# Mixture-of-experts rows: from accumulating scatters into HBM to slot-ordered writes with gathers by node

## The chip, the core and the metric

The kernel runs on one core of a Trainium2 chip. The metric is device time in microseconds (us) of one execution; three executions of the kernel before had a median of 1533.02 us (1530.13 to 1534.28). The inputs are fixed by a seed: 625 nodes with 512 features, 10,000 edges, and about 160 MB of weights and rows moved from HBM in one execution. All arithmetic of the routed layers is float32.

## The reference

Four pairs of a graph layer and a mixture-of-experts layer ("ffn") are applied to the node rows `x`, each added to its input. Two of the expert layers, called L1 and L3, are of concern here. In both each node goes to its two best of eight experts, and the two outputs are summed with a weight per choice:

```python
# L1: relu expert, 512 -> 1024 -> 512, softmax over the two best
topk_vals, topk_idx = jax.lax.top_k(logits, K)
topk_weights = jax.nn.softmax(topk_vals, axis=-1)
h = jax.nn.relu(jnp.einsum('bsh,ehf->bsef', x, w1) + b1)
expert_out = jnp.einsum('bsef,efh->bseh', h, w2) + b2
...
# L3: silu-gated expert, 512 -> 1536 -> 512, gates renormalised over the two best
out = out + combine[:, e:e + 1] * (h @ w2[e].T)
```

After L1 come a layer norm and the graph layer L2. After L3 the kernel ends: `x + L3_ffn` is its output.

## The kernel before, in words

Nodes lie in five tiles of T = 125 rows (`NT` = 5). The experts are ranked by how many nodes chose them; `CAPS` gives a fixed capacity to each rank, and every (node, choice) pair gets a *slot*, in blocks of B = 128 slots. Blocks beyond the capacities ("overflow", up to `NO`) are worked on inside nested runtime branches `tc.If(n_over[0] > i)` (L1054); in this execution none is taken. `ITEMS` lists in which order a layer works through its ranks: in L1 rank 4, 0, then 5 and 6 merged in one block of two 64-slot halves, then 1, 2, 3, 7; in L3 rank 4, 0, 1, 2, 3, 5, 6, 7. Both layers have 13 ordinary blocks (`OVER`).

`routed` (L791) runs one such layer. `dispatch` (L640) computes slots, the node of every slot (`node`) and, by ten one-hot matmuls (L764), the gate of every slot (`gate`). Then for each item: `fetch` (L872) gathers the block's rows from HBM (`rows_hbm`) with an indirect DMA on POOL's queue; `enter` (L890) transposes them on the tensor engine; `hidden` (L899, or `hidden2` L939 for the merged item) is the first product with its activation; `back` (L995) the second. An item whose width is a multiple of 128 gets its output rows straight from `back` (L1036); for the others the output comes transposed (L1003) and `turned` (L1012) turns it, one block after each step of the *next* item's `hidden`. The weights, 1 MB a chunk, stream through a ring of nine buffers: `refill` (L863) on SP's queue brings chunk n when chunk n - 9 has been read.

What the change is about is where a block's output rows go. `give` (L976) lets DVE scale them by the slot's gate into one of two buffers `ys_out` (L981), and then issues on POOL's queue an indirect DMA that *adds* the rows to the nodes' rows in HBM (L985):

```python
nc.vector.tensor_scalar(y[:n], ps[:n, 0, :], over[0][:n, b:b + 1], None, op0=OP.mult)
...
nc.gpsimd.indirect_dma_start(
    out=sums[layer], in_=y[:n], in_offset=None, compute_op=OP.add, ...)
```

All these scatters write one HBM tensor, so each waits for the one before. `keep` (L1087) first puts `x` there. In L1 that tensor is `sums`, and after the layer L1684 and L1685 read it back to `x` tile by tile, `LayerNorm.add` (L328) and `close` (L345) normalise it, and `to_features` (L388) feeds L2's first matmuls (`mm_nodes`, L455); 24 idle matmuls (`warm(24)`, L1679, which the trace shows as 48 records) keep the tensor engine busy meanwhile. In L3 the tensor is the kernel's output itself.

The order of the instructions on an engine is made by a scheduler when the program is built: of the instructions that its own cost estimates hold to be ready it takes the one that comes first in the program. On the chip each engine then runs its list strictly in order. `tc.issue_after(i)` forces instructions behind `i` on its engine. A `tc.If` is a fence for the scheduler: nothing crosses it. PSUM has four buffers of two banks.

Of the kernel before, what the change touches and what calls it, by code (L numbers as in the profile page):

```python
# [11 lines left out]
F32 = mybir.dt.float32  # L12
# [7 lines left out]
P = 128  # L20
# [27 lines left out]

ITEMS = {"L1": ((4,), (0,), (5, 6), (1,), (2,), (3,), (7,)),
         "L3": ((4,), (0,), (1,), (2,), (3,), (5,), (6,), (7,))}  # L50
# [145 lines left out]
def kernel(  # L196
# [443 lines left out]
    def dispatch(layer, o12, weigh, w0, per, dp, oh0):  # L640

        mask = dp.tile([T, NT, E], BF16, tag="mask", name="mask")
        nc.vector.tensor_add(mask, o12[:, 0], o12[:, 1])
# [99 lines left out]
        nc.vector.tensor_scalar(free, one, 0.0, spare, op0=OP.is_equal, op1=OP.mult)  # L746
        node = small.tile([P, NB], I32, tag="node", name="node")
        node_made = nc.vector.scalar_tensor_tensor(node, one, -1.0, free, op0=OP.add, op1=OP.add)
        yield node

        with tc.issue_after(node_made.ins):
            g12 = weigh()

            rest = dp.tile([T, 2 * NT], F32, tag="rest", name="rest")
            nc.vector.tensor_copy(rest, g12.rearrange("p c t -> p (c t)"))
            gates = dp.tile([T, 2 * NT, 3, NB], BF16, tag="gates", name="gates")
            piece = dp.tile([T, 3, 2 * NT], BF16, tag="piece", name="piece")
            for i in range(3):
                nc.vector.tensor_copy(piece[:, i, :], rest)
                if i < 2:  # L760
                    nc.vector.tensor_sub(rest, rest, piece[:, i, :])
                nc.vector.tensor_mul(gates[:, :, i, :], ohb, bcast(piece[:, i, :], NB))
        for n in range(2 * NT):
            pe["last"] = nc.tensor.matmul(ps[:, 1, :3 * NB], ohp[:, n, :],  # L764
                                          gates[:, n].rearrange("p i b -> p (i b)"),
                                          start=(n == 0), stop=(n == 2 * NT - 1))
        gate = small.tile([P, NB], F32, tag="gate", name="gate")
        last = nc.vector.tensor_reduce(gate, ps[:, 1, :3 * NB].rearrange("p (i b) -> p b i", b=NB),
                                axis=AX.X, op=OP.add)
        with tc.issue_after(last.ins):  # L770

            nc.vector.tensor_add(ovb, ovb, nov)
            le = dp.tile([P, NO, E], F32, tag="le", name="le")
            nc.vector.tensor_tensor(le, ovb[:, None, :].to_broadcast([P, NO, E]),
                                    blk[:, :NO, None].to_broadcast([P, NO, E]), op=OP.is_le)
            own = dp.tile([P, NO], F32, tag="own", name="own")
            nc.vector.tensor_reduce(own, le, axis=AX.X, op=OP.add)
            nc.vector.tensor_scalar(own, own, float(E - 1), None, op0=OP.min)
            whose = small.tile([P, NO, E], F32, tag="whose", name="whose")
            nc.vector.tensor_tensor(whose, own[:, :, None].to_broadcast([P, NO, E]),  # L780
                                    eio[:, None, :].to_broadcast([P, NO, E]), op=OP.is_equal)
            routing[layer, "over"] = small.tile([1, NO + 1], I32, tag="ovr_i", name="ovr_i")
            nc.vector.tensor_scalar(routing[layer, "over"][:, :NO], own[0:1, :], float(per),
                                    float(w0), op0=OP.mult, op1=OP.add)
            nc.vector.tensor_copy(routing[layer, "over"][:, NO:], ovb[0:1, E - 1:])
        pe["picked"] = last
        yield gate, whose

    HALVES = (slice(0, B // 2), slice(B // 2, B))

    def routed(layer, lg, rows, nch, nw, activate, vectors=lambda *_: None, rest=lambda *_: ()):  # L791

# [9 lines left out]
        with tc.tile_pool(name=f"{layer}w", bufs=1) as more, \  # L802
# [15 lines left out]
            yT = rpool.tile([P, KD, tall], F32, name="yT")  # L818
            beyond = rpool.tile([P, 2], I32, name="beyond")
            nc.gpsimd.memset(beyond, 0)  # L820
            nc.gpsimd.memset(beyond[B // 2:, 0:1], 2 * N)
            nc.gpsimd.memset(beyond[:B // 2, 1:2], 2 * N)
            brought, counts = {"n": 0}, {"xg": 0, "y": 0}
# [110 lines left out]
            def bias_of(i, m=0):  # L934
                if i < ni:
                    return vectors(ranks[:, :, items[i][m]], pool)
                return vectors(over[1][:, i - ni, :], pool)

# [36 lines left out]

            def give(b, n, ps, parts=None, later=None):  # L976


                y = ys_out[counts["y"] % len(ys_out)]
                counts["y"] += 1  # L980
                nc.vector.tensor_scalar(y[:n], ps[:n, 0, :], over[0][:n, b:b + 1], None, op0=OP.mult)  # L981

                def added():
                    for at_nodes in parts or (nodes[0][:n, b:b + 1],):
                        nc.gpsimd.indirect_dma_start(  # L985
                            out=sums[layer], in_=y[:n], in_offset=None, compute_op=OP.add,
                            out_offset=bass.IndirectOffsetOnAxis(ap=at_nodes, axis=0),
                            bounds_check=N - 1, oob_is_err=False)

                if later is None:  # L990
                    added()
                else:
                    later.append(added)

            def back(i, between):  # L995
# [25 lines left out]
                else:  # L1021
                    for m, (b, rows) in enumerate(blocks(i)):
                        ps = pstile("ps_y")
                        for f in range(nf):
# [13 lines left out]
                            if m == n // B - 1:  # L1038
                                done(i, f)
                        if i < ni and len(items[i]) > 1:  # L1040

                            by_half = pool.tile([P, 2], I32, tag="half", name="half")
                            nc.vector.tensor_tensor(by_half,
                                                    nodes[0][:, b:b + 1].to_broadcast([P, 2]),
                                                    beyond, op=OP.add)
                            give(b, rows, ps, [by_half[:, j:j + 1] for j in range(2)])
                        else:
                            give(b, rows, ps, later=todo if i == 0 else None)
                return todo

            def overflow(i):

                if i < NO:
                    with tc.If(n_over[0] > i):  # L1054
                        enter(ni + i)
                        if i + 1 < NO:
                            fetch(ni + i + 1)
                        hidden(ni + i, [])
                        back(ni + i, [])
                        overflow(i + 1)  # L1060

            n_over, over = [], []
            warm(4)
            o12, g12, weigh = choose(lg)
            oh0 = yT.rearrange("p k s -> p (k s)")[:T, :NT * B].rearrange("p (t s) -> p t s", t=NT)
            steps = dispatch(layer, o12, weigh, w0, per, dp, oh0)
# [11 lines left out]
            def weights_of_blocks():  # L1078
# [5 lines left out]
                after.pop(0)() if after else None  # L1084
                after.append(keep)

            def keep():  # L1087
                for part, hbm in by_node(sums[layer]):
                    nc.scalar.dma_start(hbm, x[part])

            after = []
            todo = [None, None, rows_of_others, None, weights_of_blocks]
            for i in range(ni):
                hidden(i, todo)
                ahead = [lambda: enter(i + 1), lambda: fetch(i + 2)] if i + 1 < ni else []
                todo = back(i, ahead)
                if i == 0:
                    todo = after + todo
            assert not todo
            pe["picked"] = None  # L1100
            overflow(0)
        state["stop"] = len(plan)

# [321 lines left out]
    rows_hbm = tc.dram_tile([N + B, D], F32, name="rows_hbm")  # L1425
    sums = {"L1": tc.dram_tile([N, D], F32, name="sums"), "L3": out}
    with tc.tile_pool(name="empty", bufs=1) as pool:
        empty = pool.tile([B, D], F32, name="empty")
        nc.gpsimd.memset(empty, 0.0)
        nc.gpsimd.dma_start(rows_hbm[N:N + B, :], empty)  # L1430

    prio = const.tile([T, E], F32, name="prio")
# [244 lines left out]

    routed("L1", lg, xn, 2, 1, l1_activate, l1_vectors, l1_rest)
    warm(24, behind=False)  # L1679
    xn = ktile("xn")  # L1680
    ln = LayerNorm(xn, groups=GROUPS)
    for t in range(NT):
        hbm = sums["L1"][t * T:(t + 1) * T, :]
        nc.sync.dma_start(x[:112, t, :], hbm[:112, :])  # L1684
        nc.scalar.dma_start(x[112:T, t, :], hbm[112:T, :])  # L1685
        ln.add(t, x[:, t, :])
    xnT = to_features(xn, "xnT")

# [102 lines left out]

    routed("L3", lg, xn, 3, 2, l3_activate)

# [30 lines left out]
```

## Time and profile before

| | |
|---|---|
| median of 3 runs | 1533.02 us (1530.13 to 1534.28) |
| the profiled execution | 1532.33 us, of which its span is 1530.5 us |
| TensorE busy / mean granted clock | 94% of the span / 0.978 |
| DVE, ACT, POOL busy | 43%, 25%, 14% |
| L1 routed, with its selection | about 714 to 915 us of the span |
| L3 routed, with its selection | about 1126 us to the end |
| scatters (L985) | 27, median 5.8 us from issue to landing |
| gathers of rows (L876) | 26, median 7.3 us |

PE is the tensor engine's matmuls, PEld its weight loads, DVE the vector engine, ACT the scalar engine, POOL the GpSimd engine, SP the sync engine; a q behind a name (SPq) means the engine's queue. A row of the timeline reads: start, duration, engine, line, operation, output<-input, shape, count; in brackets how long the engine was idle before it and what ended the idle time. An fp32 matmul shows as two records, so counts of records are twice the counts in the code.

### The profile page before, as it was taken

The numbers are of one execution on the slowest core, as the hardware profiler recorded it, in microseconds if no ns is written. First come the engines' busy times: TensorE is split into PE (matmuls) and PEld (weight loads), VectorE is DVE, ScalarE is ACT, GpSimd is POOL, SyncE is SP. The second block draws the span as 40 slices with busy tenths as digits, with TensorE's granted clock in tenths as the row PEclk, the third lists the DMA queues.
The fourth block names the chain that finished last, engine by engine and source line by source line (L and its number), as shares of the span: only waits on it lengthen the run. The fifth ranks groups of instructions, "written<-read, shape, count | busy, mean of one in ns | idle before, by whom it ended". The sixth has DMA issues, their size and how long they took to land.

```text
span 1530.5 us, 18483 instructions
## 1 busy us (share of the span) xinstructions
PE 1442.2 (94%) x7068; PEld 1011.3 (66%) x7068; DVE 660.9 (43%) x1752; ACT 388.6 (25%) x768; POOL 215.7 (14%) x355
## 2 busy tenths in 40 slices
PE   9998999999999999987998999799979999999996
PEld 6775556647566655655655886555558668999885
DVE  9845563372985538747411115846362101111100
ACT  2223272121564126622110105512131000011000
POOL 1010041300242013400212111100001001101000
PEclk9999999999999999998999999899989999999998
DMA  4010100021100110001966523000039416457880
GB/s 151 12 35 30 67 15 28 28 83 33 50 1 1 55 55 1 1 1 62 396 220 224 170 37 128 28 28 28 0 127 409 180 67 209 156 185 265 300 295 4
DMA packets 29057, 159.41 MB, mean 104 GB/s; under 512 B 4073, under 2 KB 4201, under 8 KB 12065
## 3 DMA queue, kind: packets, MB, share of 16 engines
q1 hardware_dynamic: 20791, 141.56, 25.2%
q0 software_dynamic: 5424, 11.32, 3.4%
q10 hardware_dynamic: 2746, 5.25, 1.1%
q8 instruction: 59, 0.97, 0.3%
q14 instruction: 37, 0.30, 0.1%
HBM read 166.49 MB, written 11.58 MB: 116 GB/s over the span
## 4 chain that ended last, share of the span: by engine, by line
PE 73%; DVE 10%; DMA 6%; issue 6%; ACT 4%; POOL 0%; SPq 0%; ACTq 0%; POOLq 0%; DVEq 0%
PE ps_h L916 16%; PE ps_mf L447 14%; PE ps_mn L455 7%; PE ps_y L1003 7%; PE ps_s L1165 5%; DMA sums<-slots,node 5%; PE ps_o L1229 4%; PE ps_eo L1119 4%; PE ps_a L1332 3%; PE ps_p L1208 3%; PE ps_mg L436 3%; PE ps_y L1036 2%; DVE s L1171 1%; PE ps_tr L397 1%; DMA slots<-rows_hbm,node 1%
## 5 line engine op out<-in xcount | busy, mean ns | idle before, releaser
L916 PE MATMUL ps_h<-xgT,ring 128*128 128x128 f32 (+5 forms) x1920 | 322.4, 328 | 4.0 <-DVE slots L981 3.9
L916 PEld LDWEIGHTS ps_h<-xgT,ring 128*128 128x128 f32 x1920 | 278.3, 192 | 45.5 <-issue 6.8
L1194 POOL TENSOR_SCALAR s<-s,rs 125x625 f32<-125x625 f32 (+4 forms) x120 | 96.3, 818 | 309.3 <-DVE rs L1191 286.6
L1003 PE MATMUL ps_y<-hT,ring 128*128 128x352 f32 (+4 forms) x640 | 137.0, 373 | 0.0
L1003 PEld LDWEIGHTS ps_y<-hT,ring 128*128 128x128 f32 x640 | 108.7, 190 | 24.3 <-issue 0.2
L1790 DVE TENSOR_TENSOR hT<-ps_h,g 128x512 f32<-128x512 f32 (+4 forms) x60 | 27.8, 464 | 197.4 <-ACT g L1789 191.0
L1176 ACT ACTIVATE s<-s,mn 125x626 f32<-125x626 f32 (+4 forms) x120 | 87.4, 745 | 62.1 <-DVE mn L1171 62.1
L1171 DVE CUSTOM_DVE_ANT_0 s<-ps_s,mask 125x626 f32<-125x626 f32 (+4 forms) x120 | 82.1, 718 | 31.7 <-PE ps_s L1165 30.8
L1165 PE MATMUL ps_s<-kT,qT 64*125 64x313 f32 (+4 forms) x416 | 84.5, 458 | 5.1 <-DVE mn L1171 5.1
L1789 ACT ACTIVATE g<-ps_h 128x512 f32<-128x512 f32 (+4 forms) x60 | 25.0, 417 | 250.7 <-PE ps_h L916 250.7
L876 POOL DMA_INDIRECT slots<-rows_hbm,node x26 | 25.5, 980 | 375.1 <-PE ps_x L894 198.1
L1208 PEld LDWEIGHTS ps_p<-ident,s 125*125 125x125 f32 x432 | 53.0, 192 | 29.1 <-issue 15.0
L1186 DVE SCALAR_TENSOR_TENSOR s<-s,cnt 125x626 f32<-125x626 f32 x80 | 66.2, 846 | 12.3 <-ACT s L1176 12.2
L1119 PE MATMUL ps_eo<-w,h 128*125 128x512 f32 x160 | 70.5, 593 | 0.6 <-ACT h L1115 0.6
L1229 PE MATMUL ps_o<-pT,v 125*64 125x375 f32 (+2 forms) x448 | 60.2, 413 | 9.1 <-DVE mn L1171 4.7
L1208 PE MATMUL ps_p<-ident,s 125*125 125x125 f32 x432 | 63.8, 290 | 4.2 <-DVE mn L1171 1.7
L1165 PEld LDWEIGHTS ps_s<-kT,qT 64*125 64x125 f32 x416 | 43.7, 186 | 32.2 <-DVE mn L1171 11.8
L386 PE MATMUL ps_warm<-rows,ident 128*128 128x313 f32 x202 | 60.4, 455 | 1.0 <-DVEq L1054 1.0
L1036 PE MATMUL ps_y<-ring,hT 128*128 128x512 f32 x128 | 58.3, 605 | 0.0
L1332 PE MATMUL ps_a<-dst,src 125*128 125x313 f16 x400 | 54.9, 297 | 1.4 <-DVE dst L1318 1.0
L1119 PEld LDWEIGHTS ps_eo<-w,h 128*125 128x125 f32 x160 | 29.8, 188 | 36.4 <-issue 30.9
L455 PE MATMUL ps_mn<-w,hxT 128*125 128x512 f32 x120 | 52.0, 593 | 0.6 <-ACT hxT L277 0.6
(414 smaller groups left out, 1978.6 us busy)
## 6 DMA issues: line engine op xcount, KB each, us to landing
ring<-in_weights SPq DMA_DIRECT2D x122, 1024.0 KB
w<-in_weights SPq DMA_DIRECT2D x27, 1024.0 KB
rows_hbm<-xn ACTq DMA_DIRECT2D x2, 1120.0 KB
x<-in_x SPq DMA_DIRECT2D x1, 1120.0 KB
sums<-x ACTq DMA_DIRECT2D x1, 1120.0 KB
x<-sums SPq DMA_DIRECT2D x5, 224.0 KB
out<-x ACTq DMA_DIRECT2D x1, 1120.0 KB
rows<-in_rows SPq DMA_DIRECT2D x1, 1052.0 KB
```

The lines of the kernel that those rows point to most:

```text
L447: pe["last"] = nc.tensor.matmul(ps[:, half, :HC], w, r[:, half * HC:(half + 1) * HC], start=(n == 0), stop=(n == last))
L455: pe["last"] = nc.tensor.matmul(ps[:T, 0, :width], src[:, k, t * T:(t + 1) * T], w[:, k, :width], start=(k == 0), stop=(k == KD - 1 and ex ...
L916: pe["last"] = nc.tensor.matmul(ps[:, m, g * n:(g + 1) * n], w[:, k, j * P:(j + 1) * P], xgT[:, k, :n], start=(k == 0), stop=(k == KD - 1))
L1003: nc.tensor.matmul(ps[:, 0, :n], second(i, f)[:, d * P:(d + 1) * P], hT[:, f, :n], start=(f == 0), stop=(f == nf - 1))
L1036: nc.tensor.matmul(ps[:, 0, :], hT[:, f, m * B:m * B + rows], second(i, f), start=(f == 0), stop=(f == nf - 1))
L1119: pe["last"] = nc.tensor.matmul(ps[:T, 0, :], hs[e][:, t * T:(t + 1) * T], ws[e // 4][1][:, e % 4, :], start=True, stop=True)
L1165: nc.tensor.matmul(ps[hh][:T, i, :w], qT[rr, b, t * T:(t + 1) * T], kT[rr, b, i * w:(i + 1) * w], start=True, stop=True)
L1171: nc.vector.tensor_tensor_reduce(s[:, hh, :nb * w].rearrange("p (a c) -> p a c", a=nb), ps[hh][:T, :nb, :w], mask[:, t, :nb * w].rearrange ...
L1194: nc.gpsimd.tensor_scalar(s[:, hh, :w], s[:, hh, :w], rs[:, hh:hh + 1], 1.0, op0=OP.mult, op1=OP.mult)
L1208: nc.tensor.transpose(pp[:T, hh, j * T:(j + 1) * T], s[:, hh, j * T:(j + 1) * T], ident[:T, :T])
L1229: nc.tensor.matmul(po[rr, 0, o:n * T], v[:, j, h * DH:(h + 1) * DH], pT[:, hh, j, o:n * T], start=(j == 0), stop=(j == nk - 1))
L1332: nc.tensor.matmul(pa[b // 2][:, b % 2, :HC], srcs[c % SRCS][:, b, :], dsts[c][:, :HC], start=(c == c0), stop=(c == c1 - 1))
```

## The change

Routed outputs no longer go through accumulating scatters.

- **Ordinary blocks but the last.** `give` copies the rows unscaled on ACT to `ys_out`, and an ordinary DMA on ACT's queue writes them to `ys_hbm` at the block's slots.
- **Nodes fetch theirs.** Before the last item's `hidden`, `picked_up` issues ten indirect gathers on POOL (five node tiles by two choices, 125 rows each) from `ys_hbm`, and DVE adds each to `x` with the node's gate. A choice that lies in the last block or in overflow is pointed at a row of zeros. In L1 the last two of the ten additions are held back until `spread`.
- **The last block (and overflow).** `one_hots` builds five 128 x 125 one-hot matrices on DVE; `spread` multiplies each with the block's rows on the tensor engine (K = 128, 512 columns), and DVE adds the product, times the gate, to `x`. The call for the last ordinary block stands behind the overflow branches.
- **After a node tile is complete** a callback runs: in L1 its layer-norm statistics (tiles 0 and 2 on ACT, the others on DVE), in L3 the DMAs of the tile to the output. `keep` and the reading back of `sums` are gone; `warm(24)` becomes `warm(4)`.
- **In `dispatch`** the three-piece gates, their ten matmuls and the reduction are gone; a clamped slot number, one product and one sum come in.
- **Order.** In L1 the merged item (5, 6) moves from third to sixth place. Overflow rows are fetched inside the branch. At the program's start ten small DMAs on POOL put zeros to the unused rows of `ys_hbm`.

```diff
-ITEMS = {"L1": ((4,), (0,), (5, 6), (1,), (2,), (3,), (7,)),
+ITEMS = {"L1": ((4,), (0,), (1,), (2,), (3,), (5, 6), (7,)),
...
-        for n in range(2 * NT):
-            pe["last"] = nc.tensor.matmul(ps[:, 1, :3 * NB], ohp[:, n, :],
-                                          gates[:, n].rearrange("p i b -> p (i b)"),
-                                          start=(n == 0), stop=(n == 2 * NT - 1))
-        gate = small.tile([P, NB], F32, tag="gate", name="gate")
...
+            nc.vector.tensor_scalar(from_hbm, slot, B * (OVER[layer] - 1), None, op0=OP.min)
...
+            nc.vector.tensor_mul(by_choice, ohb[:, :, late],
+                                 bcast(g12.rearrange("p c t -> p (c t)"), NO + 1))
+            gate = small.tile([T, NT, NO + 1], F32, tag="gate", name="gate", bufs=1)
+            last = nc.vector.tensor_add(gate, by_choice[:, :NT, :], by_choice[:, NT:, :])
...
-            def give(b, n, ps, parts=None, later=None):
+            def give(b, n, ps):
                 y = ys_out[counts["y"] % len(ys_out)]
-                counts["y"] += 1
-                nc.vector.tensor_scalar(y[:n], ps[:n, 0, :], over[0][:n, b:b + 1], None, op0=OP.mult)
...
+                if b < over0:
+                    counts["y"] += 1
+                nc.scalar.copy(y[:n], ps[:n, 0, :])
+                if b < over0 - 1:
+                    nc.scalar.dma_start(ys_hbm[layer][B * b:B * b + n, :], y[:n])
                 else:
+                    kept.append((b, y))
+
+            def picked_up():
...
+                for n in order:
+                    nc.gpsimd.indirect_dma_start(
+                        out=places[n], out_offset=None, in_=ys_hbm[layer],
+                        in_offset=bass.IndirectOffsetOnAxis(ap=over[0][:, n:n + 1], axis=0))
+                def add(n):
+                    c, t = divmod(n, NT)
+                    nc.vector.scalar_tensor_tensor(x[:, t, :], places[n], weights_of[0][:, c, t:t + 1],
+                                                   x[:, t, :], op0=OP.mult, op1=OP.add)
+                for n in order[:-2]:
+                    add(n)
+                return [lambda n=n: add(n) for n in order[-2:]]
+
+            def one_hots(b):
...
+                for t in range(NT):
+                    nc.vector.tensor_scalar(ohT[:, t, :], place[:, :T], float(t * T), number,
+                                            op0=OP.add, op1=OP.is_equal)
+                return ohT
+
+            def spread(ohT, remain=(), done=lambda t: None):
+                b, y = kept.pop()
+                for t in range(NT):
+                    ps = pstile("ps_sp")
+                    pe["last"] = nc.tensor.matmul(ps[:T, 0, :], ohT[:, t, :], y, start=True, stop=True)
+                    if t == NT - 1 and remain:
+                        with tc.issue_after(last.ins):
+                            while remain:
+                                remain.pop(0)()
+                    j = b - over0 + 1
+                    last = nc.vector.scalar_tensor_tensor(x[:, t, :], ps[:T, 0, :], over[1][:, t, j:j + 1],
+                                                          x[:, t, :], op0=OP.mult, op1=OP.add)
+                    done(t)
...
             for i in range(ni):
+                if i == ni - 1:
+                    assert not todo
+                    remain = picked_up()
+                    if nw > 1:
+                        while remain:
+                            remain.pop()()
+                    ohT = one_hots(over0 - 1)
                 hidden(i, todo)
...
             overflow(0)
+            kept.append(last)
+            spread(ohT, remain, lambda t: complete(t, spares[0][:, t, :]))
...
-    warm(24, behind=False)
-    xn = ktile("xn")
-    ln = LayerNorm(xn, groups=GROUPS)
-    for t in range(NT):
-        hbm = sums["L1"][t * T:(t + 1) * T, :]
-        nc.sync.dma_start(x[:112, t, :], hbm[:112, :])
-        nc.scalar.dma_start(x[112:T, t, :], hbm[112:T, :])
-        ln.add(t, x[:, t, :])
+    def l1_complete(t, spare):
+        if t == 0:
+            l2["xn"] = ktile("xn")
+            l2["ln"] = LayerNorm(l2["xn"], groups=GROUPS)
+        l2["ln"].add(t, x[:, t, :], t in (0, 2), spare)
+
+    routed("L1", lg, xn, 2, 1, l1_activate, l1_complete, l1_vectors, l1_rest)
+    warm(4)
...
+    def l3_complete(t, _):
+        hbm = out[t * T:(t + 1) * T, :]
+        nc.sync.dma_start(hbm[:112, :], x[:112, t, :])
+        nc.scalar.dma_start(hbm[112:, :], x[112:T, t, :])
```

## The prediction, made before the result was known

> **What bounds the kernel now.** I read the page first, then what PE waits for in the two routed stages, then the timeline around each such wait and around each stage's end.
>
> ```profile
> PE 1442.2 (94%) x7068; PEld 1011.3 (66%) x7068; DVE 660.9 (43%) x1752; ACT 388.6 (25%) x768; POOL 215.7 (14%) x355
> ```
>
> PE is busy 94%. The granted clock is what differs inside that, so I asked for stretches (columns: stretch, its length, PE, PEld, DVE, ACT, POOL busy, clock, DMA share, GB/s):
>
> ```profile
> 819.15:825.20 6.05, 6.05 (x11) 3.55 (x12) 0.93 (x2) 0.56 (x1) 2.69 (x2) 0.50 0.34 67
> 825.20:834.00 8.80, 8.80 (x31) 5.71 (x30) 1.17 (x2) 0.56 (x1) 1.80 (x2) 1.00 0.51 140
> ...
> 1143.00:1510.00 367.00, 366.81 (x2142) 313.35 (x2143) 52.51 (x133) 34.12 (x79) 31.12 (x25) 1.00 0.62 221
> ```
>
> L3's body has no idle PE at all (366.81 of 367): nothing taken off DVE or POOL there can pay. L1's body has one large hole, told by PE's waits in 720 to 915 us and the timeline:
>
> ```profile
> PE ps_h L916 <- DVE slots L981: 3.9, 1, 3.9
> ```
>
> ```profile
> 818.34 0.75 DVE L981 TENSOR_SCALAR slots<-ps_y,gate 128x512 f32<-128x512 f32 x1 [9.19 <-DMA sums<-slots,node]
> 819.01 1.07 DVE L1656 TENSOR_SCALAR hT<-ps_h,bias 128x352 f32<-128x352 f32 x2
> ...
> 819.15 15.10 PE L916 MATMUL ps_h<-xgT,ring 128*128 128x352 f32 x40 [3.89 <-DVE slots L981]
> ```
>
> DVE waits 9.19 us for a scatter to release a `ys_out` buffer; the activations L1656 stand behind it, PSUM fills, PE idles 3.89 us and then runs 11 records in 6.05 us at clock 0.50, where the same shape takes 8.80/31 = 0.284 us at 1.00. That is 6.05 - 11 x 0.284 = 2.9 us more. The stages' ends are latency:
>
> ```profile
> 909.41 0.75 DVE L981 TENSOR_SCALAR slots<-ps_y,gate 128x512 f32<-128x512 f32 x1 [6.12 <-PE ps_y L1036]
> ...
> 910.44 1.55 POOL L985 DMA_INDIRECT sums<-slots,node  x1 [6.67 <-DVEq L1054]
> 915.22 3.17 SPq L1684 DMA_DIRECT2D x<-sums  x5
> ...
> 918.11 0.69 DVE L339 BATCH_NORM_STATS2 ln_st<-x 125x6 f32<-125x512 f32 x1 [7.95 <-DMA x<-sums]
> ...
> 926.89 3.32 PE L455 MATMUL ps_mn<-w,xnT 128*125 128x288 f32 x13
> ```
>
> L1: last product 909.4, scatter, reading back, norm, L2's first product 926.89: 17.5 us. L3, from the timeline and the sequencer's rows of L1054 (the branch's exit) and L1820 (the end):
>
> ```profile
> 1518.24 0.75 DVE L981 TENSOR_SCALAR slots<-ps_y,gate 128x512 f32<-128x512 f32 x1 [8.98 <-PE ps_y L1036]
> 1519.26 1.56 POOL L985 DMA_INDIRECT out<-slots,node  x1 [30.19 <-DVEq L1054]
> ```
>
> ```profile
> L1054 POOLq INC_SWDGE_SEM  x2: 760/1004/1247, 914.3 to 1523.9; - x2
> ```
>
> ```profile
> L1820 POOLq DRAIN  x3: 46/107/4481, 1525.1 to 1530.2; - x3
> ```
>
> Last product 1518.24, scatter landed about 1523.6, then on POOL 1.25 us at the branch's exit and a drain of 4.48 us, end 1530.5: 12.3 us.
>
> **The change, part by part**, against 1532.33 us. T0 is a layer's last product, Th the start of its last item's `hidden` (L1: T0 = Th + 15.2; L3: Th = 1486.3, T0 = Th + 32).
>
> *The hole in L1.* No scatter is left. ACT's copy (0.6 us as L275's 128x512 copies) can still wait for a buffer: it is freed by a plain 256 KB write, for which the nearest row is the 224 KB read-back, 2.9 us from issue (915.22) to reader (918.11). The third block of an item comes 4 us after the first where the next item is 176 wide (steps 855.6, 857.3, 858.9), so ACT waits at most about 1 us; the 2.7 us that DVE waited there (861.78) did not idle PE. Gain 3.9 + 2.9 = 6.8; bounds 0 (ACT takes over the wait) and 7.6 (the 0.8 us PE gap at 807 goes too).
>
> *L1's end.* Rows: ACT copy 0.6; a product 0.6; L1121's update of `x` from PSUM 0.75; statistics 0.69 + 0.18. From T0: first update at T0 + 1.3; DVE then does 5 updates (3.75), 2 held additions (2 x 0.73 as L1639 = 1.46), three statistics (2.6): T0 + 9.1. ACT's two (1.9 each) and its table load of 1.28 end before that. From the last statistics (922.68) to 926.89 were 4.2: T0 + 13.3 in place of 17.5, gain 4.2. The branch's exit does not delay it: PE's came 3.3 us early in its queue before.
>
> Held additions need gathers. Each occupies POOL 0.97 plus 0.3 (1179.60, 1180.87, 1182.10). Landing from these rows:
>
> ```profile
> DMA to landing us min/median/max: 3.0/7.3/11.0
> ```
>
> The median is from full DMA engines; where they were mostly idle (839 to 850) it was 3.3, and L1's end was at 0.17 share. [...] With the block's write landed at Th + 3.5, gather k lands at Th + 6.8 + 1.27k by the row: k = 7 at Th + 15.7, k = 9 at Th + 18.2 = T0 + 3.0, before DVE asks at T0 + 6. [...] I take the row: 0.
>
> Eight additions precede the last item's activations in the program. [...] I charge 1.0, bounds 0 and 12 (all eight ahead, below).
>
> *Warming.* `warm(24)` covers PE until 923; `warm(4)` ends about T0 + 5.3, and the first transposes come at about T0 + 9.8: 4.5 us idle, longer than the 3.89 above. [...] I take the row: +1.3, bounds 0 and 3.
>
> *L3's end.* First update T0 + 1.3, five updates to 5.1, the last tile's DMA 2.9 as above: T0 + 8.0; the final barrier after the drain took 0.9 (1529.6 to 1530.5): T0 + 8.9 against 12.3. POOL has nothing after the gathers, so exit and drain (5.7) run beside `back`; if they wait for T0 they end at T0 + 6.5, still covered. Gain 3.4; without the cover (drain after the output's landing) a loss of 2.3.
>
> *L3's last item.* All ten additions precede its activations (Th + 8.0, 15.1, 22.3). The write lands at Th + 5 (weights still stream to 1490), gather k at Th + 8.3 + 1.27k, the last at 19.7. Each activation is held by 2 us at most; `back` starts at Th + 21.4, 1.4 us after the last addition. 0; if gathers take the median, 3.
>
> *Gates.* Ten products (0.45 us, L764) go. L3: -0.45. In L1 PE waits 1.8 us for gathers right after, which takes it up: 0. DVE's lost 1.9 us there end at no PE wait.
>
> *Order.* The merged item needs eight chunks in one go; it had the DMA engines at 396 GB/s at 808 to 815. Late, chunks 20 to 27 follow reads spread over some 40 us of items (2) and (3), so 200 GB/s: no wait, 0.
>
> *Zeros at the start.* Ten POOL DMAs of 0.8 to 1 us after 73.4 put L1264 to about 84; ACT's L1269 waits, but its product is needed in the next layer, and `rc` (84.7), which may share their buffer, moves by 2 us where PE has about 8 us of PSUM slack. 0, bounds 0 and 3.
>
> *ACT* gains 26 copies, about 16 us at 25% load, in stages where it idles 250 us for L916: 0. `keep`'s writes go: 0, nothing waited for them.
>
> Sum: -6.8 - 4.2 + 1.0 + 1.3 - 3.4 - 0.45 = -12.55: 1519.8. The profiled execution is 0.7 under the median, so 1520.5.
>
> **The rivals.** (a) As summed, 1520.5. The removed waits and two shorter tails speak for it. (b) Half of it: the hole stays because ACT waits in DVE's stead, or POOL's drain stays exposed: 1520.5 + 6.8 = 1527.3, or + 5.7 = 1526.2. For: ACT feeds half of L1's activations. Against: a plain write is half a scatter's way. (c) Slower: the additions stand ahead of all activations in DVE's queue in both last items. L1: eight additions end at Th + 16.5, `hidden` ended at Th + 8: PE idles 8.5, then half clock 3, some 11.5. L3: with busy gathers the last addition at Th + 24, `back` 4 us late plus 3. Together 18.5, less the 1.0 charged: 1538. It decides once the stalls exceed the gains of about 14 us. For: the scheduler put L981 ahead of ready activations before. Against: it estimates a landing too, and the first activation is ready before any gather. (d) More than summed: neither the 1.0 nor the 1.3 falls due, and the 0.8 us gap at 807 goes: 1520.5 - 3.1 = 1517.4. (e) The branch fence serialises more than it did: 1531, no change.
>
> **How the numbers follow.** (a) 0.48, (b) 0.25, (c) 0.09, (d) 0.10, (e) 0.08. A measurement can tell about 0.3% (4.6 us) from no change. Faster is (a), (b), (d): 0.83; same 0.08; slower 0.09. The range goes from (d) with room for a shorter L1 end, 1513, to (e), 1531, and leaves (c) out.
>
> **What would show it.** PE's waits in L1 no longer name DVE's or ACT's block copies; clock 1.00 where 0.50 stood. First L2 product 13 to 14 us after L1's last; end 9 us after L3's. POOL's drain of 4.5 us ahead of T0. I am wrong if PE waits for DVE in the last items with additions ahead, if ACT's copies wait over 3 us for writes, or if PE starts L2 at half clock for more than 6 us.

## The result and the profile after

The changed kernel takes 1538.66 us (median of 6 runs, 1537.72 to 1540.89) where the kernel before, on the same chip, takes 1533.65 (6 runs, 1530.13 to 1535.34): ratio 1.0038 [1.0027, 1.005]. It is slower, by 0.4%; 1520.5 had been predicted. The profiled execution took 1540.89 us, its span is 1538.5; it is the slowest of the six, so the table below loses 8.0 us where the medians lose 5.0.

The stages, in us, from the first and last PE records of each in the two traces, one execution each (Th and T0 as in the prediction):

| stage | before | after | difference | predicted |
|---|---|---|---|---|
| start to L1's first product | 725.1 | 727.1 | +2.0 | 0 |
| L1's body, to Th | 169.2 | 162.4 | -6.8 | -6.8 |
| L1's last item, Th to T0 | 15.0 | 16.6 | +1.6 | +1.0 |
| L1's end, T0 to L2's first product | 17.5 | 27.7 | +10.2 | -2.9 |
| L2 to L3's first product | 216.3 | 212.4 | -3.9 | 0 |
| L3's body, to Th | 343.1 | 342.7 | -0.4 | -0.45 |
| L3's last item, Th to T0 | 31.9 | 38.8 | +6.9 | 0 |
| L3's end | 12.3 | 10.7 | -1.6 | -3.4 |
| sum | | | +8.0 | -12.55 |

What was to be gained in L1's body came in full, and 3.9 us came ahead of L3 where the prediction had put nothing. The gain is given back at two places, and PE's waits over the whole run name both (what waited, for whom, us in total, times, longest):

```profile
PE ps_sp L1022 <- DVEq L1083: 11.4, 1, 11.4
...
PE ps_y L1073 <- DVE hT L1839: 4.1, 1, 4.1
```

By stretches (columns as in the prediction), the body of L1 has 5.5 us of idle PE left in 170, and the loss sits in the 28 us after L1's last product, at clock 0.70:

```profile
720.00:890.00 170.00, 164.47 (x838) 120.05 (x838) 38.60 (x134) 25.79 (x55) 14.62 (x28) 0.99 0.62 228
...
906.00:934.00 28.00, 13.64 (x40) 7.71 (x40) 13.67 (x34) 8.48 (x18) 2.60 (x4) 0.70 0.48 150
1146.00:1489.00 343.00, 342.73 (x1934) 290.47 (x1935) 41.74 (x117) 38.69 (x87) 11.36 (x12) 1.00 0.63 232
1489.00:1528.00 39.00, 34.73 (x217) 26.67 (x215) 9.38 (x13) 2.54 (x5) 12.33 (x10) 0.91 0.39 111
```

The timeline of L1's end in the changed kernel, in order of time:

```profile
902.45 3.70 PE L1073 MATMUL ps_y<-ring,hT 128*128 128x512 f32 x8 [2.03 <-ACT hT L1700]
...
907.64 3.04 SPq L249 DMA_DIRECT2D w<-in_weights  x3
...
910.22 0.75 DVE L998 SCALAR_TENSOR_TENSOR x<-spare,g,x 125x512 f32<-125x512 f32 x1 [0.79 <-DMA spare<-ys_hbmL,fromh]
...
917.52 7.03 PE L1022 MATMUL ps_sp<-slots,yT 128*125 128x512 f32 x10 [11.37 <-DVEq L1083]
...
919.59 0.75 DVE L1028 SCALAR_TENSOR_TENSOR x<-ps_sp,gate,x 125x512 f32<-125x512 f32 x1 [8.63 <-PE ps_sp L1022]
...
933.82 6.47 PE L457 MATMUL ps_mn<-w,xnT 128*125 128x288 f32 x26
```

The last product ends at 906.15. DVE is still adding gathered rows and comes to the branch with the eighth, at 910.2. Only at 917.4 is it out of the branch (L1083), as the sequencer's rows tell (shortest, median, longest in ns, then the first and the last start; the first is L1's):

```profile
L1083 DVEq COMPARE_BRANCH  x2: 63/70/76, 910.2 to 1516.7; - x2
L1083 POOLq INC_SWDGE_SEM  x2: 862/1067/1272, 915.0 to 1514.3; - x2
L1083 DVEq EVENT_SEMAPHORE  x2: 21/21/21, 917.4 to 1518.7; - x2
```

So the end of L1 is 4.1 to the branch, 7.1 in it, 2.2 to the first update, 8.7 for updates, additions and statistics (to 928.25), 5.6 for the rest of the norm and the transposes. Beside it lies something new on SP: L2's three weight loads, 1 MB each, start at 907.64. Before, they stood behind the read-backs of `sums` in SP's queue and left at 918.99, 9.6 us after the last product and not 1.5; there is no read-back any more for them to stand behind.

In L3's last item (the timelines of POOL, DVE and PE, by time):

```profile
1496.22 1.20 POOL L992 DMA_INDIRECT slots<-ys_hbmL,fromh  x1 [123.48 <-DMA ys_hbmL<-slots]
...
1502.19 0.78 DVE L998 SCALAR_TENSOR_TENSOR x<-slots,g,x 125x512 f32<-125x512 f32 x1 [22.41 <-DMA slots<-ys_hbmL,fromh]
...
1515.92 1.54 DVE L998 SCALAR_TENSOR_TENSOR x<-spare,g,x 125x512 f32<-125x512 f32 x2 [2.46 <-DMA spare<-ys_hbmL,fromh]
1517.37 1.28 DVE L1839 TENSOR_TENSOR hT<-ps_h,g 128x512 f32<-128x512 f32 x2
1518.11 9.69 PE L1073 MATMUL ps_y<-ring,hT 128*128 128x512 f32 x16 [4.07 <-DVE hT L1839]
```

The second of the item's three activations was ready when ACT's half of it ended (1504.33 + 0.60 = 1504.9). It stands behind the last seven additions in DVE's queue, and runs with the third at 1517.37, after the last gather. PE idles 4.07 us, and the clock is at 0.5 from 1516.5 for 6.8 us.

### The profile page after: what moved, and what is told of

It reads as the page before. It is cut to its first block, busy times and chain, and to the rows that moved or that the text cites. A ratio compares the mean times of both kernels' runs of the same rounds, so it can differ in the third digit from the quotient of the medians.

```text
span 1538.5 us, 18460 instructions
## 1 busy us (share of the span) xinstructions
PE 1441.3 (94%) x7028; PEld 1007.6 (65%) x7028; DVE 663.5 (43%) x1749; ACT 404.7 (26%) x804; POOL 200.6 (13%) x350
## 5 line engine op out<-in xcount | busy, mean ns | idle before, releaser
L910 PE MATMUL ps_h<-xgT,ring 128*128 128x128 f32 (+5 forms) x1920 | 318.6, 326 | 0.1
L1040 PEld LDWEIGHTS ps_y<-hT,ring 128*128 128x128 f32 x640 | 108.8, 190 | 24.4
L1227 DVE SCALAR_TENSOR_TENSOR s<-s,cnt 125x626 f32<-125x626 f32 x80 | 66.2, 846 | 12.2 <-ACT s L1217 12.1
L1206 PEld LDWEIGHTS ps_s<-kT,qT 64*125 64x125 f32 x416 | 43.7, 185 | 32.5 <-DVE mn L1212 12.1
L449 PE MATMUL ps_mf<-xnT,w 128*128 128x313 f32 x192 | 51.7, 426 | 0.0
```

The lines of the kernel that those rows point to most:

```text
L910: pe["last"] = nc.tensor.matmul(ps[:, m, g * n:(g + 1) * n], w[:, k, j * P:(j + 1) * P], xgT[:, k, :n], start=(k == 0), stop=(k == KD - 1))
L1040: nc.tensor.matmul(ps[:, 0, :n], second(i, f)[:, d * P:(d + 1) * P], hT[:, f, :n], start=(f == 0), stop=(f == nf - 1))
L1206: nc.tensor.matmul(ps[hh][:T, i, :w], qT[rr, b, t * T:(t + 1) * T], kT[rr, b, i * w:(i + 1) * w], start=True, stop=True)
L1227: nc.vector.scalar_tensor_tensor(s[:, hh, :], s[:, hh, :], 1.0, counts[:, t, :], op0=OP.mult, op1=OP.mult, accum_out=sm[:, hh:hh + 1])
```

## The experiments

Ten kernels, each compared with the kernel before on its chip (1532.95, 1532.19 and 1533.06 us in the three groups). The letters of the theories hold within one expectation.

**e1_late_w**: SP holds L2's loads until L1's first update, by a 16-byte DMA that reads `x`.

```diff
-        wbc, wres = take(2)
+        hold = tc.dram_tile([1, 4], F32, name="hold")
+        held = nc.sync.dma_start(hold, x[0:1, 0, :4])
+        with tc.issue_after(held.ins):
+            wbc, wres = take(2)
```

> The kernel after, with L2's three weight loads held on SP's queue behind L1's first update of x from the one-hot products (a 16-byte DMA of x goes ahead of them). In the kernel after, L1's last product ends at 906.15 us and L2's first starts at 933.82 (27.7 us; 17.5 before): DVE's eight additions wait for gathers until 910.97, then DVE stands 6.4 us at the branch's exit. [...] Theory B (the exit waits for POOL's, that is for all gathers, whatever the DMA load): DVE's exit still comes behind POOL's, L1's end takes 22 us or more, 1533 or more.

1533.27 us, ratio 1.0005 [0.9996, 1.0013]; L1's end 24.0 in place of 27.7. The sequencer's rows of this kernel:

```profile
L1083 DVEq COMPARE_BRANCH  x2: 63/70/76, 910.4 to 1510.4; - x2
...
L1083 DVEq EVENT_SEMAPHORE  x2: 21/21/21, 913.5 to 1512.4; - x2
```

DVE reaches the branch as late as before the edit (910.4) but leaves it after 3.1 us, not 7.1: 4.0 of the loss belong to the loads. The trace's DMA records hint how: an 8 KB read, on a queue that carries none of the program's tensors and that the page lists as `q14 instruction`, precedes the exit by 1.8 to 2.1 us where DVE reaches the branch late (it starts at 915.3 in the changed kernel, 911.7 in this one, 910.8 in e4_both), and with the loads ahead it starts 5.1 us after the branch, without them 1.0 to 1.3. By the queue's name I take it for a read of instructions; that it is DVE's, or that DVE waited for it, no run shows, as the records name no engine. By its numbers this is theory B's outcome: DVE's exit comes 0.3 us behind POOL's (913.53 and 913.22), the end takes over 22 us and the run over 1533. But in e9_adds_after_exit below DVE's exit did not wait for POOL's (897.0 and 910.9). Theory A had the gathers land sooner with no loads beside them, DVE out of the branch within 1 us of its last addition, L1's end at 17 to 19 us and the run near 1529. It failed in its gathers: they came no earlier without the loads, so that DVE still reached the branch 4.3 us after the last product.

One caution on the totals: 3.7 us of what this trace saves over the changed kernel's are in L3's last item, which the edit does not touch (35.1 us here, 37.8 in e2_no_branch, 38.8 in the changed kernel). PE's pause there was 2.98 us here and no half clock came with it; at 3.98 us it came for 3.4 us, at 4.07 for 6.8.

**e2_no_branch**: the call of `overflow(0)` left out in both layers.

> The kernel after without the branches over overflow blocks in L1 and L3 (the code that would work on overflow blocks is left out; none is taken with these inputs, so the same rows are computed). The loads stay early. Theory A: the 6.4 us at DVE's exit go, the slow gathers stay: first update about 5 us after L1's last product, L1's end 20 to 22 us, L3's end about 1 us shorter, the run 6 to 8 us less than after, about 1531. Rival C (the branch has no part in it, the late gathers alone hold DVE): L1's end stays at 26 us or more, the run within 2 us of after.

1532.69 us, ratio 0.9999 [0.999, 1.0008]; L1's end 22.5, a little above what theory A allowed and well below C. The branch costs 5.2 (27.7 less 22.5). The loads still cost something, I take it, now at one of the two additions that were held back (its gather, the ninth, was issued at 905.03, 13.1 us before; in e4_both, with no loads beside it, the ninth landed 5.3 us after its start):

```profile
918.14 0.75 DVE L998 SCALAR_TENSOR_TENSOR x<-spare,g,x 125x512 f32<-125x512 f32 x1 [4.78 <-DMA spare<-ys_hbmL,fromh]
```

**e3_adds_l3**: L3's ten additions issued behind the last item's activations.

```diff
-                for n in order[:-2]:
-                    add(n)
-                return [lambda n=n: add(n) for n in order[-2:]]
+                return [lambda n=n: add(n) for n in order]
...
-                    if nw > 1:
-                        while remain:
-                            remain.pop()()
+                    if layer not in ('L3',):
+                        while len(remain) > (0 if nw > 1 else 2):
+                            remain.pop(0)()
...
                 hidden(i, todo)
+                if i == ni - 1 and layer in ('L3',):
+                    with tc.issue_after(pe["act"].ins):
+                        while len(remain) > (0 if nw > 1 else 2):
+                            remain.pop(0)()
```

> The kernel after with L3's ten additions of gathered rows placed behind the three activations of the last item on DVE; L1 as it was. In the kernel after, L3's last item takes 38.8 us from 1489.0 to 1527.8 (31.9 before): PE waits 4.1 us for an activation that stands behind additions, then runs 6.8 us at half clock. Theory D (the order on DVE alone): PE's wait and the half clock go, the item takes 32 us, the run 6 to 7 us less, about 1532. Rival E (gathers that start 7 us into the item are too late in any order, so the additions now hold the first update from the one-hot products): PE's wait goes, but L3's end grows by as much, the run within 2 us of after.

1531.59 us, ratio 0.9998 [0.999, 1.0005]; L3's last item 31.9, as before the change, and L3's end 10.5. DVE's timeline shows the third activation on time and the additions behind it:

```profile
1510.62 0.69 DVE L1841 TENSOR_TENSOR hT<-ps_h,g 128x512 f32<-128x512 f32 x1 [6.46 <-ACT g L1840]
1511.23 2.07 DVE L998 SCALAR_TENSOR_TENSOR x<-slots,g,x 125x512 f32<-125x512 f32 x3
```

The whole 6.9 us of that stage was the order in one queue; in the traces of e1 and e2, with the old order, it was 3.2 and 5.9.

**e4_both**: e1's hold, and e3's edit in L3 and (for the first eight additions) in L1.

> The kernel after with both edits (loads of L2's weights held back; additions behind the last activation, eight in L1 and ten in L3). If A and D hold, the gains add up: 10 in L1's end, 2 in L1's last item, 7 in L3's last item, so about 1520, faster than both kernels. If L1's additions, now later, hold the updates from the one-hot products instead, L1's end takes 2 to 3 us more and the run is near 1523. If B and E hold, 1535 or more.

1527.76 us, ratio 0.9961 [0.9947, 0.9975]: faster than both kernels. L1's last item is 14.3, L3's 31.9, but L1's end still 24.4, so it missed the expected 1520 to 1523. DVE is at the branch at 909.8, 5.6 after the last product, because the gathers follow each other by 1.5 us and the eighth is only then there.

**e5_order**: the kernel before with the new `ITEMS` of L1 and nothing else.

```diff
-ITEMS = {"L1": ((4,), (0,), (5, 6), (1,), (2,), (3,), (7,)),
+ITEMS = {"L1": ((4,), (0,), (1,), (2,), (3,), (5, 6), (7,)),
```

> The kernel before with one edit: in L1 the item of two experts comes sixth, as in the change. No expert is left out, only the order moves. Theory F (the 6.8 us that L1's body lost belonged to the scatters, whatever the order): L1 from its first x product to the last item's start stays within 168 to 172 us with a hole elsewhere, and the run stays at 1533 to 1536. Theory G (the old order made the hole, where three blocks came 4 us apart): 162 to 164 us and the run near 1526, so the reorder alone would have earned it.

1527.64 us, ratio 0.9975 [0.9964, 0.9985]; L1's body 162.5, its last item 14.3, its end 18.5. With all scatters in place the hole is gone. DVE still waits for a scatter, 3.54 us at the longest, but PE does not idle (timeline of DVE, then two stretches):

```profile
840.66 0.75 DVE L981 TENSOR_SCALAR slots<-ps_t,gate 96x512 f32<-96x512 f32 x1 [3.54 <-DMA sums<-slots,node]
```

```profile
820.00:840.00 20.00, 20.00 (x96) 15.30 (x95) 2.95 (x5) 1.27 (x3) 2.40 (x2) 1.00 0.44 135
840.00:862.00 22.00, 22.00 (x156) 21.55 (x155) 5.62 (x12) 2.88 (x8) 6.62 (x5) 1.00 0.83 245
```

So the reorder by itself takes out the 6.8 of the body, with 4.6 left of it in the run's medians (1532.19 to 1527.64). The opposite, the changed kernel in the old order, was not tried: its pick-up wants no block left to turn when the last item starts. Whether the plain writes alone would have closed the hole stays open.

**e6_both_no_branch**: e4_both without the overflow branches.

> The kernel of e4_both with the overflow branch left out of both routed layers (rows over the capacity would be lost; these inputs have none). Theory A (in e4_both L1's end is 24.4 us because DVE gets to the branch only after the gathered rows are added, 5.6 us after the last product, and leaves it 2.9 us later): PE spreads right after ACT's copy, the clock stays full, and the last gather, some 8 us after the last product, is what is left: L1's end 16 to 18 us, the run 1520 to 1522. Rival C (half clock and the norm's chain hold it): L1's end 22 or more, the run 1525 or more.

1521.54 us, ratio 0.9935 [0.9918, 0.9951]; L1's end 18.6 (expected 16 to 18). The clock stays at 1.00 until the transposes, at 919.5. Even with no branch and no loads beside it this end is no shorter than the scatter's (17.5 before; 18.5 and 17.9 in e5_order and e10_mixed, in the new order): DVE waits 2.6 us for gathers, until 908.01, T0 + 4.

**e8_both_warm and e11_warm14**: e4_both with `warm(28)`, and then `warm(14)`, ahead of the branch in L1.

> The kernel of e4_both with 28 dummy products on PE between L1's last product and the branch, some 8 us at full clock, so that PE does not idle while it waits for DVE. Theory C (part of L1's end is half clock: updates 1.48 us apart where 0.75 would do, transposes slower): the spread and its updates run at full clock and L1's end falls from 24.4 to 20 to 22 us, the run to 1524 to 1526. Rival (the wait at the branch alone decides, since the held additions and the norm follow anyway): L1's end within 0.7 of 24.4, the run 1527 to 1528.

> The kernel of e8_both_warm with 14 dummy products in place of 28: each of them is two records of 0.27 us, so 28 took 14.9 us, past DVE's exit from the branch at 8.1 us after the last product; 14 take 7.5. Theory C sized by e8_both_warm (from the first update to L2's first product 12.8 us at full clock where e4_both took 13.6): L1's end 23 to 24 us in place of 24.4, the run some 1 us under e4_both. Rival (the wait alone): 24.4 and more.

e8: 1531.19 us, ratio 1.0 [0.9991, 1.0009], L1's end 29.0. I had mis-sized it: 28 dummy products took 14.9 us, past DVE's exit. e11: 1526.79 us, ratio 0.9961 [0.9948, 0.9975], L1's end 22.9 in place of 24.4 (timeline of PE):

```profile
905.13 7.54 PE L388 MATMUL ps_warm<-rows,ident 128*128 128x313 f32 x28
914.18 4.53 PE L1020 MATMUL ps_sp<-slots,yT 128*125 128x512 f32 x10 [1.52 <-DVEq L1081]
```

The spread's ten records take 4.53 us here and 6.10 in e4_both. So half clock is worth 1.5 us of that end in these two traces (the medians differ by 1.0, which their intervals can't tell from nothing); the wait is the larger part.

**e9_adds_after_exit**: e4_both with L1's ten additions behind the branch, two after each tile's update.

> The kernel of e4_both with L1's ten additions moved behind the branch's exit in DVE's queue, two after each tile's update (rows over the capacity would overwrite gathered rows; these inputs have none). Theory A: DVE reaches the branch before the last product, its exit costs nothing at the end, first update 1.5 to 2.5 us after the last product, then the last gather is what is left: L1's end 16 to 18 us, the run 1519 to 1522. Rival B (the exit waits for POOL, which waits for the last gather, wherever the additions stand): PE still waits 6 us or more for the branch, L1's end 23 or more, the run 1526 or more.

1528.18 us, ratio 0.9974 [0.9967, 0.9981]; L1's end 25.7. The sequencer's rows of the branch, and DVE's timeline:

```profile
L1086 DVEq COMPARE_BRANCH  x2: 63/70/76, 896.3 to 1511.8; - x2
L1086 DVEq EVENT_SEMAPHORE  x2: 21/21/21, 897.0 to 1512.6; - x2
...
L1086 POOLq INC_SWDGE_SEM  x2: 862/1067/1272, 910.9 to 1507.5; - x2
```

```profile
904.89 0.75 DVE L1027 SCALAR_TENSOR_TENSOR x<-ps_sp,gate,x 125x512 f32<-125x512 f32 x1 [7.96 <-PE ps_sp L1021]
911.85 1.54 DVE L999 SCALAR_TENSOR_TENSOR x<-slots,g,x 125x512 f32<-125x512 f32 x2 [6.21 <-DMA spare<-ys_hbmL,fromh]
```

DVE's exit did not wait for POOL's: 897.0 against 910.9. The first update comes at T0 + 1.9. But the first addition then waits to 911.85, though its rows landed at 897.7 and in e4_both such rows were added before 903. POOL's last step in the branch ran from 910.87 to 910.87 + 0.86 = 911.73; it began when the ninth gather had landed (910.76), and DVE's wait ended at its end. I take the wait for one for POOL's exit; the tenth gather landed at 911.64, so the times alone do not exclude it. Both theories held by half, and the stall moved from the branch to the addition.

**e10_mixed**: L1 as before in the new order, L3 as in e3_adds_l3.

> L1 as in the kernel before (scatters, reading back, 24 dummy products) but in the new order, L3 as in the change with its additions behind the activations. All work is done. Theory (the change earns in L3's end alone, and the L1 half of it only loses): L1's body 162.5, L1's end 18.5 as in e5_order, L3's body 342.7 in place of 343.1, its end 10.4 in place of 12.2, so some 2.2 us under e5_order's 1527.6: 1524.5 to 1526.5. Rival (the two halves are tied, by DMA or by memory, or the stage between gives it back): 1527 or more.

1519.77 us, ratio 0.9918 [0.9904, 0.9931]: the fastest of all, and all work is done. L1's end 17.9, L3's last item 31.9, L3's end 10.6. It beat the expectation by 4.7 us; its trace has 4.5 less than e5_order's in the stage from L2 to L3 (211.5 against 216.0), which no edit was meant for (see `keep` below).

## Why the prediction was wrong

**L1's end: the step that failed most.** It read "The branch's exit does not delay it: PE's came 3.3 us early in its queue before." I looked at PE's exit; the one that counts is DVE's, and the change puts eight additions, each with a gather to wait for, ahead of it. It was DVE's exit that PE waited for before the change, too, though for 1 us only (timeline of PE, before):

```profile
910.36 12.88 PE L386 MATMUL ps_warm<-rows,ident 128*128 128x313 f32 x48 [0.99 <-DVEq L1054]
```

The first update came at T0 + 13.4 where I had T0 + 1.3. That is 12.1 of the 13.1 us missed here; the rest of the chain was about right (14.2 with its half clock, 13.3 predicted). Of the 12.1, 4.0 are the weight loads (e1_late_w). The prediction moved a step past SP's queue without noticing: with `sums` gone, the loads came 8 us earlier after T0, into the gathers and the exit.

**The gathers, mis-sized.** I had a pitch of 1.27 us and a landing 3.3 us after the start. These gathers took 1.20 us on POOL with 0.3 between, a pitch of 1.5, and in L1 landed 5.6 us after their start (the eighth: 904.54 to 910.15); in e4_both, with no loads beside them, 5.3 (the ninth: 905.70 to 911.02). So the eighth was there at Th + 20.6, not Th + 15.7, and the ninth at Th + 25.3 beside the loads (21.2 in e4_both), not 17.0. Less POOL's 1.2, the ninth's transfer in e4_both took 4.1. The busy median of 7.3, which I had set aside, was 1.7 to 2.0 too long, and the row 2.0 to 2.3 too short.

**L3's last item: failed.** It read "Each activation is held by 2 us at most" and came to 0. I had the write landed at Th + 5 and the last gather at Th + 19.7. The write was issued at Th + 0.8 and the first gather started at Th + 7.2, 6.4 us later, while weights streamed; with the pitch of 1.5 and a landing of 5.9 the last two additions ran at Th + 26.9. PE then waited 4.1 and ran 2.8 us longer for half clock, 6.9 in all (e3_adds_l3 takes out exactly that). Rival (c) had this part nearly word for word, "`back` 4 us late plus 3".

**Rival (c), 1538, got the total.** But only its L3 half happened. In L1 the additions held PE up for 2.0 us at the activations, not 11.5. Nor does any run show the 1.0 that I had charged there: the last item took 16.6 us after 15.0, and 14.3 in e4_both with eight additions behind the activations. The loss was behind them, at the branch, which rival (e) alone had named. Of the signs of being wrong one came: PE waited for DVE in a last item with additions ahead.

**L1's body: right in size, not in reason.** I wrote that the hole goes because "No scatter is left". e5_order shows that the order alone does it, and I had costed *Order* at 0: a benefit of it I had not looked for. That the term hit its -6.8 is luck.

**`keep`, put at nothing.** I wrote "`keep`'s writes go: 0, nothing waited for them." In the trace of before, L3's two writes of `x` stand among ACT's instructions of the norm ahead of L3 (timelines of ACT and PE before, by time; then ACT after):

```profile
1121.49 0.30 ACT L290 ACTIVATE rs_s<-ln_mv,eps 125x3 f32<-125x3 f32 x1
1123.29 0.82 ACT L367 ACTIVATE xn<-x,ln_nb,ln_r 125x512 f32<-125x512 f32 x1 [1.50 <-DVE ln_nb L364]
1123.99 0.34 ACTq L1089 DMA_DIRECT2D out<-x  x1
1124.01 0.28 ACT L290 ACTIVATE rs_s<-ln_mv,eps 125x2 f32<-125x2 f32 x1
...
1126.32 1.92 PE L397 MATMUL ps_tr<-ident,xn 125*128 125x125 f32 x8 [1.09 <-DVE ln_nb L364]
```

```profile
1127.19 0.53 ACT L292 ACTIVATE rs_s<-ln_mv,eps 125x3 f32<-125x3 f32 x2
```

Before, the square root for the last two tiles (L290) stands behind a tile's normalisation, which itself waits for DVE, and behind the second write: it runs 2.5 us after the one for the first three. After, the two follow each other at once. DVE needs that root for its scale factors, so PE waits 1.09 us more in the transposes, and a half clock of 6.8 us falls on them and on L3's selection. The two traces with `keep` in L3 (before, e5_order) have that order, that wait, that half clock and 216.3 and 216.0 us from L2 to L3's first product; the ten without have none of the three, and 210.9 to 212.5. No run puts the writes alone back, so that they make the order is argued.

**Right:** the gates (-0.4), ACT's copies (no wait of PE names them in L1), POOL's drain covered in L3, the merged item's late fetch (PE's waits for gathered rows in L1 are 2.3 us).

**L3's end, mis-sized:** 10.7, not 8.9. The first update comes at T0 + 1.9, not 1.3, the five go at the spread's pace, 4.19 us and not 3.75, and the last output DMA is issued 6.4 us after T0:

```profile
1529.69 4.19 DVE L1028 SCALAR_TENSOR_TENSOR x<-ps_sp,gate,x 125x512 f32<-125x512 f32 x5 [11.03 <-PE ps_sp L1022]
...
1531.45 2.76 SPq L1843 DMA_DIRECT2D out<-x  x5
```

**Warming, mis-sized with its cause.** 1.3 was my estimate for a pause of 4.5 us, and no run shows that term: the pause became 11.4. After PE's restart at 917.52 the clock stayed at 0.5 until 922.55, 5.0 us; after L3's stall 5.2. My row had 6.05, 0.9 to 1.0 too long.

**What stays open.** The mean clock from L2 to L3's first product is 0.94 before and 0.97 after. Ahead of L3 it is at 0.5 for 6.8 us before (at 1125.6) and in e5_order (at 1120.9), and for 0 to 3.4 us there in the ten with L3 changed. Why those ten spread over 1.6 us, no run tells. The start's +2.0 is no effect of the change: e5_order, with the start of before, had 727.2 as well, and all runs lie between 725.1 and 728.8.

## What to carry to other kernels

When a wait is taken away, list every instruction that stood behind it, in every queue: here weight loads slipped 8 us forward into the transfers that now mattered. On DVE an addition that waited for its gather held what stood behind it: an activation, for which PE idled 4.07 us in L3's last item, and the way through the branch, for which PE waited 11.37 us in L1. So activations that the critical engine needs, and an engine's way through a branch, belong ahead of such a wait; one edit of order gave back 6.9 us. And before a large rewrite of a stall, try the smallest edit of its order alone: one line in `ITEMS` took out the 6.8 us of L1's body that the whole rewrite had been credited with, and with the half of the change that pays (L3's) it makes the fastest kernel. Of what that half adds over e5_order in the traces (9.1 us, 1.8 of them the start's own variation), 4.5 lie where two writes fell away that had been put at nothing: before a term is put at 0, look at what stands behind the instruction in its queue.

## What the runs showed of the hardware

- In L1, DVE's way out of the branch, which wasn't taken, took 0.7 to 0.8 us, in which its last operation was still running, where DVE came there early or without additions ahead (e9_adds_after_exit, before), 2.9 to 3.1 where it came late (e4_both, e1_late_w), and 7.1 with 3 MB of loads just issued (changed kernel). An 8 KB read on the queue listed as `q14 instruction` started 1.8 to 2.1 us ahead of these three late exits; whose read it was, the records don't say.
- A wait for a gather that was put behind a branch lasted until POOL was out of it (6.21 us in e9_adds_after_exit, for rows that had landed); that POOL's exit is what it waited for is argued.
- A pause of PE of 2.98 us left the clock at 1.00 (e1_late_w, L3's last item); one of 3.98 in the same place came with half clock for 3.4 us (e2_no_branch), one of 4.07 for 6.8 (changed kernel).
- A gather of 125 rows took POOL 1.20 us in the median, one of 128 rows from another tensor 0.95 to 0.98 by the pages' means. The reason was not looked for.
